# A graph block on one core: keys' and values' products placed between attention's gathers, the next head's maxima spread over a head, rows by DRAM, 16-bit routing

## The chip, the cores and the metric

The kernel runs on one core of one Trainium2 chip. The metric is device time in microseconds (us) of a whole execution. The engines are named as in the profile: PE multiplies matrices (PEld is its weight load), DVE is the vector engine, ACT the scalar engine with the exponential, POOL is GpSimd, SP is the engine that issues most DMAs.

## The reference, cut to what matters

x has 1250 nodes of 768 features, and src, dst hold 41,250 edges. Everything is fp32.

```python
xn = layernorm(x)
# 1. two graph attention layers (4 heads of 192, then 2 of 96), on a second layer norm of xn
h = (x @ W).reshape(n, H, C)
e = leaky_relu(s_src[src] + s_dst[dst], 0.2)      # s_src, s_dst: one number a node and head
ee = exp(e - segment_max(e, dst)[dst])
out = segment_sum(ee / denom[dst] * h[src], dst) + bias
gnn = concatenate([x, out2]) @ Wu + bu
# 2. linear attention, 12 heads of 64, phi = elu + 1
kv, ksum = einsum(phi(k), v), phi(k).sum()
mix = (phi(q) @ kv / (phi(q) @ ksum)) @ Wo + bo
x = x + gnn + mix
# 3. eight experts, two a token, gates not normalised
gate = layernorm(x) @ Wg + bg
scores, idx = top_k(gate, 2)
x = x + sum over the two of score * (gelu(xl @ W1[e] + b1[e]) @ W2[e] + b2[e])
```

## The kernel before, in words

Nodes are cut into ten tiles of 125 (PT, NT). The whole kernel is straight code, traced once; a scheduler orders each engine's instructions by their place in the program and by when it thinks that they are ready. So an instruction can run long before those that are written ahead of it, where its inputs and buffers allow that. The trace shows the order that results.

The stages are these.

1. Edges become a dense matrix of counts AT (source tile by all 1250 targets) and its mask. The normalised nodes, transposed (xnT), are multiplied by weights folded from W1 and W2 (L430), which gives gw, what is gathered, and s1, the two scores of each node and head.
2. Attention, six heads in two layers. `attend` (L495) treats one head. `across` (L497) lays a column of scores over all partitions as a row of 1250: ten PE transposes, up to four in one PSUM bank, three evacuations by ACT. There is one such bank (rb_p, L475). It makes ss_row, the sources' scores less the head's least one. Ten DVE operations (L515) then take, for each target tile, the maximum of ss_row under the mask. From those come two columns, up and dn (L523, L524), and two more rows by `across`. The loop over source tiles st (L528) makes a weight tile w of 125 x 1250: two exponentials on ACT (L533, L534), a maximum and a multiplication by the counts on DVE (L535, L536). w has three buffers, v two. A gather multiplies w on PE: in layer one w is the stationary side, ten blocks times 198 columns (L548); in layer two h2 is (L569). The sums take five PSUM banks in layer one, and after each head DVE adds them, divided by the denominator, into h2 (L555 to L558); after a head of layer two ACT copies them to o2T (L574).
3. Four weight buffers are opened once attention's memory is closed (L581, L584): Wo, Wq, Wu, and a smaller one for the rest of Wu (L591, L593).
4. Keys and values (L598 to L629): for each node tile and half (k) six matmuls for keys, six for values, then three that multiply the two, added to kvacc by DVE. In the trace an fp32 matmul is two instructions, so a half is 12, 12 and 6. Keys pass through elu + 1: add, minimum, an exponential on ACT, maximum and add.
5. kvacc is masked, transposed and multiplied into Wo (L637 to L684).
6. Routing (L768): for each node tile, queries (L751) of the next tile, the output rows po (L781, L792), a layer norm, gates (L810), rank among the eight, and from it counts of earlier nodes per expert (L830, with tri, ones and cum), a place for each of the two choices, and one-hot matrices hot and put (L849, L852), whose product inv (L854) inverts places into node numbers and gates. idx and gs (L859, L861) hold these.
7. Experts (L950): rows of xl_d are gathered from DRAM by idx, transposed, pass two layers, are scaled by gs and added into the output by an indirect DMA.

Of the kernel before, what the change touches and what calls it, by code (L numbers as in the profile page):

```python
# [69 lines left out]
def gps_block(ctx: ExitStack, tc: tile.TileContext, x, src, dst, norm_g, norm_b, W1, a_src1, a_dst1,  # L70
# [60 lines left out]
    xl_d = dram.tile([N + 128, D], F32)  # L131
# [348 lines left out]
    def least(ss, H):  # L480

        mn = small.tile([PT, H], F32, name="mn")
        nc.vector.tensor_reduce(mn, ss.rearrange("p t h -> p h t"), AX.X, ALU.min)
        p = four()
        nc.tensor.transpose(p[:H, 0], mn, ident[:PT, :PT])
        m1 = small.tile([H, 1], F32, name="m1")
        nc.vector.tensor_reduce(m1, p[:H, 0], AX.X, ALU.min)
        p = four()
        nc.tensor.transpose(p[:, 0, :H], m1.to_broadcast([H, PT]), ident[:H, :H])
        lo = small.tile([PT, 2, H], F32, name="lo")  # L490
        nc.vector.tensor_copy(lo[:, 0], p[:, 0, :H])
        nc.vector.tensor_scalar(lo[:, 1], p[:, 0, :H], -1.0, None, op0=ALU.mult)
        return lo

    def attend(ss, sd, lo, wp, rb, gather):  # L495

        def across(cols, name, bufs, bias=0.0):  # L497

            row = rb.tile([PT, N], F32, name=name, bufs=bufs)
            for g0 in range(0, NT, 4):  # L500
                n = min(4, NT - g0)
                p = four()
                for q in range(n):
                    nc.tensor.transpose(p[:, q], cols[:, g0 + q:g0 + q + 1].to_broadcast([PT, PT]),
                                        ident[:PT, :PT])
                nc.scalar.activation(row[:, g0 * PT:(g0 + n) * PT],  # L506
                                     p[:, :n].rearrange("p a b -> p (a b)"), AF.Identity, bias=bias)
            return row


        ss_row = across(ss, "ss_row", 1, lo[:, 1:2])
        top = small.tile([PT, NT], F32, name="top")
        for t in range(NT):
            scr = wp.tile([PT, N], BF16, name="scr", bufs=1)
            nc.vector.tensor_tensor_reduce(scr, ss_row, mask[:, t], 1.0, 0.0, ALU.mult, ALU.max,  # L515
                                           top[:, t:t + 1])

        nc.vector.scalar_tensor_tensor(top, top, lo[:, 0:1], sd, op0=ALU.add, op1=ALU.add)
        nc.vector.scalar_tensor_tensor(top, top, SLOPE, top, op0=ALU.mult, op1=ALU.max)
        up = small.tile([PT, NT], F32, name="up")  # L520
        dn = small.tile([PT, NT], F32, name="dn")
        sl = small.tile([PT, NT], F32, name="sl")
        nc.vector.tensor_sub(up, sd, top)  # L523
        nc.vector.scalar_tensor_tensor(dn, sd, SLOPE, top, op0=ALU.mult, op1=ALU.subtract)  # L524
        nc.vector.tensor_scalar(sl, ss, SLOPE, None, op0=ALU.mult)
        up_row = across(up, "up_row", 1)
        dn_row = across(dn, "dn_row", 1)
        for st in range(NT):  # L528


            w = wp.tile([PT, N], F32, name="w", bufs=3)
            v = wp.tile([PT, N], F32, name="v", bufs=2)
            nc.scalar.activation(w, up_row, AF.Exp, bias=ss[:, st:st + 1])  # L533
            nc.scalar.activation(v, dn_row, AF.Exp, bias=sl[:, st:st + 1])  # L534
            nc.vector.tensor_tensor(w, v, w, op=ALU.max)  # L535
            nc.vector.scalar_tensor_tensor(w, w, 2.0, AT[:, st, :N], op0=ALU.min, op1=ALU.mult)  # L536
            gather(st, w)

    lo1 = least(s1[:, :, :, 0], H1)
    with tc.tile_pool(name="wp", bufs=3) as wp, tc.tile_pool(name="rb", bufs=1) as rb:  # L540
        with tc.tile_pool(name="ag_p1", bufs=1, space=PSUM) as ag_p:
            for hd in range(H1):
                ag = ag_p.tile([PT, NT // 2, 512], F32, name="ag")

                def gather1(st, w):
# [6 lines left out]
                attend(s1[:, :, hd, 0], s1[:, :, hd, 1], lo1[:, :, hd], wp, rb, gather1)  # L552
                v = ag[:, :, :2 * CG].rearrange("p a (b c) -> p a b c", b=2)
                rd = small.tile([PT, NT // 2, 2, 1], F32, name="rd")
                nc.vector.reciprocal(rd, v[:, :, :, C2:C2 + 1])  # L555
                for t in range(NT):
                    nc.vector.scalar_tensor_tensor(h2[:, t], v[:, t // 2, t % 2], rd[:, t // 2, t % 2],
                                                   h2[:, t], op0=ALU.mult, op1=ALU.add)  # L558
# [3 lines left out]
        lo2 = least(h2[:, :, at:at + H2], H2)  # L562
        with tc.tile_pool(name="ag_p2", bufs=1, space=PSUM) as ag_p:
            for hd in range(H2):
                ag = ag_p.tile([C2 + 1, 3, 512], F32, name="ag")

                def gather2(st, w):
                    for i, (a, b) in enumerate(NCH):
                        nc.tensor.matmul(ag[:, i, :b - a], h2[:, st, hd * (C2 + 1):(hd + 1) * (C2 + 1)],  # L569
                                         w[:, a:b], start=st == 0, stop=st == NT - 1)  # L570

                attend(h2[:, :, at + hd], h2[:, :, at + H2 + hd], lo2[:, :, hd], wp, rb, gather2)
                for i, (a, b) in enumerate(NCH):
                    nc.scalar.copy(o2T[:, hd, a:b], ag[:, i, :b - a])  # L574
# [22 lines left out]

    for t in range(NT):  # L598
        ky = kp.tile([PT, D], F32, name="ky", bufs=2)
        va = kp.tile([PT, KC, 129], F32, name="va")  # L600
        nc.gpsimd.memset(va[:, :, 128:], 1.0)
        for k in range(2):
            half = slice(k * 384, (k + 1) * 384)
            for w in (Wk_sb, Wv_sb):
                ps = bank()
                for c in range(KC):
                    nc.tensor.matmul(ps[:PT, :384], xnT[:, c, t * PT:(t + 1) * PT], w[:, c, half],  # L607
                                     start=c == 0, stop=c == KC - 1)
                if w is Wk_sb:
                    ke = kp.tile([PT, 384], F32, name="ke", bufs=1)  # L610
                    nc.vector.tensor_add(ky[:, half], ps[:PT, :384], bk_b[:, half])
                    nc.vector.tensor_scalar(ke, ky[:, half], 0.0, None, op0=ALU.min)
                    nc.scalar.activation(ke, ke, AF.Exp)
                    nc.vector.scalar_tensor_tensor(ky[:, half], ky[:, half], 0.0, ke, op0=ALU.max,
                                                   op1=ALU.add)
                else:
                    nc.scalar.copy(va[:, 3 * k:3 * k + 3, :128],
                                   ps[:PT, :384].rearrange("p (b c) -> p b c", b=3))
            ps = bank()
            for c in range(3):  # L620
                nc.tensor.matmul(ps[:, c * 129:(c + 1) * 129],
                                 ky[:, (3 * k + c) * 128:(3 * k + c + 1) * 128], va[:, 3 * k + c],
                                 start=c == 0, stop=c == 2, skip_group_check=True)
            acc = kvacc[:, 3 * k:3 * k + 3]
            got = ps[:, :387].rearrange("p (b c) -> p b c", b=3)
            if t:
                nc.vector.tensor_add(acc, acc, got)  # L627
            else:
                nc.vector.tensor_copy(acc, got)  # L629
# [56 lines left out]
    zero = fp.tile([128, D], F32)  # L686
    nc.gpsimd.memset(zero, 0.0)
    nc.sync.dma_start(xl_d[N:], zero)
    nc.sync.dma_start(out[N:], zero)
# [4 lines left out]
    gs = fp.tile([128, NV + 1], F32)  # L694
# [4 lines left out]
    with ExitStack() as rs:  # L699
# [7 lines left out]
        def numbers(shape, pattern, base, mult, name):  # L707
            t = rp.tile(shape, F32, name=name)
# [8 lines left out]
        row128 = numbers([PT, 128], [[1, 128]], 0, 0, "row128")  # L717
        steps = numbers([128, NE, NJ - FIX], [[0, NE], [128, NJ - FIX]], 128 * FIX, 0, "steps")
        slot_row = numbers([PT, NV], [[1, NV]], 0, 0, "slot_row")
# [6 lines left out]
        ones = rp.tile([PT, 128], F32)  # L726
        nc.gpsimd.memset(ones, 1.0)
        tri = rp.tile([PT, 128], F32)
# [4 lines left out]
        nc.gpsimd.memset(gs[:, NV:], 0.0)  # L733
# [5 lines left out]
        cum = rp.tile([PT, NT + 1, NE], F32)  # L739
        nc.vector.memset(cum[:, 0], 0.0)  # L740
        inv = g_p.tile([128, 2, NV], F32, name="inv", bufs=1)
# [26 lines left out]
        for t in range(NT):  # L768
# [30 lines left out]
            xl = rl.tile([PT, D], F32, name="xl")  # L799
            normalise(xl, xt)  # L800
            for p, tt in token_rows(t):
                nc.sync.dma_start(xlr[p, tt], xl[p])
# [6 lines left out]
            gate = rl.tile([PT, NE], F32, name="gate")  # L809
            nc.vector.tensor_add(gate, pg[:PT, :NE], bg_b)  # L810

# [11 lines left out]
            sel = rl.tile([PT, NE], F32, name="sel")  # L823
# [10 lines left out]
            two = rl.tile([PT, 2, 2, NE], F32, name="two")  # L834
            for i, a in enumerate((at, gate)):
                nc.vector.tensor_mul(two[:, i], kth, a[:, None, :].to_broadcast([PT, 2, NE]))
            both = rl.tile([PT, 2, 2], F32, name="both")
            nc.vector.tensor_reduce(both, two, AX.X, ALU.add)
            b_i = rl.tile([PT, 2], I32, name="b_i")
            nc.vector.tensor_copy(b_i, both[:, 0])  # L840
# [6 lines left out]
            for k in range(2):  # L847
                hot = rl.tile([PT, 128], F32, name="hot")
                nc.vector.tensor_scalar(hot, row128, s_f[:, 1, k:k + 1], None, op0=ALU.is_equal)  # L849
                put = rl.tile([PT, 2, NV], F32, name="put")  # L850
# [165 lines left out]
```

## Time and profile before

| | |
|---|---|
| Median of 3 runs | 1179.99 us (1179.2 to 1181.08) |
| The profiled execution | 1180.66 us |
| Its span in the trace | 1178.6 us |
| Mean granted clock of PE | 0.971 |
| Busy | PE 91%, PE's loads 61%, DVE 57%, ACT 30%, POOL 6% |

The span is cut as follows by the trace (first starts): edges and features to some 196 us; the first maximum of attention at 220.37; the last gather's end at 593.4; the weights for the output at 612.97; routing to 937; the first gather of tokens at 937.47; experts to the end. The profile gives for each engine what it did and what ended its idle time. A busy PE need not be at its peak, because matmuls overlap: where it is, back-to-back starts tell. A clock below 1.0 means that PE was granted less than full speed.

### The profile page before, as it was taken

The numbers are of one execution on the slowest core, as the hardware profiler recorded it, in microseconds if no ns is written. First come the engines' busy times: TensorE is split into PE (matmuls) and PEld (weight loads), VectorE is DVE, ScalarE is ACT, GpSimd is POOL, SyncE is SP. The second block draws the span as 40 slices with busy tenths as digits, with TensorE's granted clock in tenths as the row PEclk, the third lists the DMA queues.
The fourth block names the chain that finished last, engine by engine and source line by source line (L and its number), as shares of the span: only waits on it lengthen the run. The fifth ranks groups of instructions, "written<-read, shape, count | busy, mean of one in ns | idle before, by whom it ended". The sixth has DMA issues, their size and how long they took to land.

```text
span 1178.6 us, 12106 instructions
## 1 busy us (share of the span) xinstructions
PE 1077.8 (91%) x4583; PEld 723.6 (61%) x4583; DVE 669.1 (57%) x1366; ACT 358.1 (30%) x527; POOL 76.3 (6%) x100
## 2 busy tenths in 40 slices
PE   2599998999999999988989999999999589999993
PEld 2586655578788878544545666666666356666652
DVE  6866666669696966687922555555555422222210
ACT  2131114373737373373712211111111011111111
POOL 1000000000000000000000000000000122322321
PEclk9999998999999999989989999999999789999997
DMA  5014000000000001000083111111123537777533
GB/s 156 27 51 163 16 25 1 1 1 1 1 1 1 1 1 53 1 0 1 1 319 103 40 40 40 40 40 40 39 65 106 191 91 188 200 209 219 121 56 54
DMA packets 33282, 79.62 MB, mean 68 GB/s; under 512 B 5258, under 2 KB 13020, under 8 KB 33208
## 3 DMA queue, kind: packets, MB, share of 16 engines
q1 hardware_dynamic: 27608, 59.02, 15.2%
q0 software_dynamic: 5600, 19.66, 8.4%
q8 instruction: 40, 0.66, 0.2%
q14 instruction: 34, 0.28, 0.1%
HBM read 60.37 MB, written 18.30 MB: 67 GB/s over the span
## 4 chain that ended last, share of the span: by engine, by line
PE 70%; DVE 20%; DMA 5%; issue 2%; ACT 2%; POOL 1%; DVEq 0%; SPq 0%; POOLq 0%; ACTq 0%
PE po L781 13%; PE ph L926 8%; PE py L938 7%; PE mm L430 7%; PE mm L607 7%; PE mm L751 7%; DVE scr L515 6%; DVE w L535 5%; DVE w L536 5%; PE ag L548 3%; PE ag L569 2%; PE u L792 2%; PE px L912 2%; PE mm L405 2%; DMA w<-in_L_gnn_Wu_dram 2%
## 5 line engine op out<-in xcount | busy, mean ns | idle before, releaser
L548 PE MATMUL ag<-kept,w 125*125 125x198 f32 x800 | 137.4, 333 | 5.1 <-DVE w L536 4.9
L548 PEld LDWEIGHTS ag<-kept,w 125*125 125x125 f32 x800 | 133.5, 188 | 9.0 <-DVE w L536 9.0
L926 PE MATMUL ph<-xsT,w 128*128 128x384 f32 (+1 forms) x324 | 100.6, 470 | 1.8 <-DVE xsT L915 1.8
L938 PE MATMUL py<-w,hT 128*128 128x384 f32 x300 | 100.6, 486 | 0.0
L430 PE MATMUL mm<-Wg,xnT 128*125 128x400 f32 x240 | 91.8, 520 | 1.0 <-DVE xnT L321 0.6
L607 PE MATMUL mm<-Wv_sb,xnT 128*125 128x384 f32 x240 | 85.7, 489 | 4.8 <-DVE kvacc L627 4.8
L535 DVE TENSOR_TENSOR w<-v,w 125x1250 f32<-125x1250 f32 x60 | 86.3, 1453 | 6.6 <-ACT w L533 5.9
L515 DVE CUSTOM_DVE_ANT_0 scr<-ss_row,mask 125x1250 bf16<-125x1250 f32 x60 | 87.2, 1453 | 0.5 <-ACT ss_row L506 0.2
L781 PE MATMUL po<-w,xnT 128*125 128x384 f32 x240 | 84.8, 496 | 2.6 <-DMA w<-in_L_gnn_Wu_dram 2.6
L536 DVE SCALAR_TENSOR_TENSOR w<-w,AT 125x1250 f32<-125x1250 f32 x60 | 86.4, 1455 | 0.4
L926 PEld LDWEIGHTS ph<-xsT,w 128*128 128x128 f32 x324 | 59.8, 193 | 41.4 <-DVE xsT L915 2.4
L607 PE MATMUL mm<-Wk_sb,xnT 128*125 128x384 f32 x240 | 84.4, 486 | 0.0
L534 ACT ACTIVATE v<-dn_row,sl 125x1250 f32<-125x1250 f32 x60 | 79.3, 1333 | 16.9 <-DVE w L535 16.4
L751 PE MATMUL mm<-w,xnT 128*125 128x384 f32 x240 | 84.2, 489 | 0.0
L915 DVE COPY xsT<-px 128x384 f32<-128x384 f32 x50 | 25.5, 552 | 99.2 <-PE px L912 77.3
L781 PE MATMUL po<-w,qT 128*125 128x384 f32 x240 | 80.8, 486 | 0.0
L938 PEld LDWEIGHTS py<-w,hT 128*128 128x128 f32 x300 | 55.3, 190 | 33.9
L941 DVE TENSOR_TENSOR ys<-py,wb 128x768 f32<-128x768 f32 x25 | 23.9, 958 | 74.0 <-PE py L938 45.5
L781 PEld LDWEIGHTS po<-w,xnT 128*125 128x125 f32 x240 | 44.2, 190 | 30.1 <-DMA w<-in_L_gnn_Wu_dram 2.8
L781 PEld LDWEIGHTS po<-w,qT 128*125 128x125 f32 x240 | 44.2, 188 | 29.4
L607 PEld LDWEIGHTS mm<-Wv_sb,xnT 128*125 128x125 f32 x240 | 42.4, 187 | 31.1 <-DVE kvacc L627 6.9
L751 PEld LDWEIGHTS mm<-w,xnT 128*125 128x125 f32 x240 | 43.6, 188 | 27.6 <-ACT qT L321 0.2
(274 smaller groups left out, 1415.6 us busy)
## 6 DMA issues: line engine op xcount, KB each, us to landing
w<-in_L_ffn_W_dram SPq DMA_DIRECT2D x18, 1152.0 KB
xt<-in_x_dram SPq DMA_DIRECT2D x20, 336.0 KB
wb<-in_L_ffn_b_dram SPq DMA_DIRECT2D x9, 384.0 KB
out_dram<-xt SPq DMA_DIRECT2D x10, 336.0 KB
xl_d<-xl SPq DMA_DIRECT2D x10, 336.0 KB
W_sb<-in_L_gnn_W_dram SPq DMA_DIRECT2D x1, 2304.0 KB
Wk_sb<-in_L_mix_Wk_dram SPq DMA_DIRECT2D x1, 2304.0 KB
Wv_sb<-in_L_mix_Wv_dram SPq DMA_DIRECT2D x1, 2304.0 KB
```

The source lines that it names most:

```text
L430: nc.tensor.matmul(ps[:PT, :2 * (CG + 2)], xnT[:, c, t * PT:(t + 1) * PT], Wg1[:, c, 2 * k:2 * k + 2].rearrange("p h c -> p (h c)"), start ...
L515: nc.vector.tensor_tensor_reduce(scr, ss_row, mask[:, t], 1.0, 0.0, ALU.mult, ALU.max, top[:, t:t + 1])
L534: nc.scalar.activation(v, dn_row, AF.Exp, bias=sl[:, st:st + 1])
L535: nc.vector.tensor_tensor(w, v, w, op=ALU.max)
L536: nc.vector.scalar_tensor_tensor(w, w, 2.0, AT[:, st, :N], op0=ALU.min, op1=ALU.mult)
L548: nc.tensor.matmul(ag[:, t // 2, o:o + CG], w[:, t * PT:(t + 1) * PT], gw[:, st, hd], start=st == 0 and t % 2 == 0, stop=st == NT - 1, ski ...
L607: nc.tensor.matmul(ps[:PT, :384], xnT[:, c, t * PT:(t + 1) * PT], w[:, c, half], start=c == 0, stop=c == KC - 1)
L751: nc.tensor.matmul(ps[:PT, :384], xnT[:, c, tk], Wq_sb[:, c, half], start=c == 0, stop=c == KC - 1)
L781: nc.tensor.matmul(po[k][:, :384], l, r[:, k * 384:(k + 1) * 384], start=i == 0, stop=i == len(parts) - 1)
L915: nc.vector.tensor_copy(xT[:, 3 * a:3 * a + 3, j * 128:(j + 1) * 128], px[:, a, :384].rearrange("p (b n) -> p b n", b=3))
L926: nc.tensor.matmul(ph[:, :n * 128], w[0][:, o:o + 128], xT[:, c, :n * 128], start=c == 0, stop=c == KC - 1)
L938: nc.tensor.matmul(py[:, k, :384], hT[:, f, j * 128:(j + 1) * 128], w[:, o:o + 384], start=f == 0, stop=f == FC - 1)
```

## The change

- `attend` becomes `layer`, over all heads of a layer. A generator `sides_of(h)` holds a head's maxima, two at a time, then its up and dn columns. The first head's is run through at once; each later head's is stepped once after each source tile of the head ahead of it: two maxima after each of tiles 0 to 4, the columns after tile 5.
- Rows: each layer's scores less the least (over) are transposed once for all heads and written to DRAM (`to_rows`); up and dn of a later head too. Later heads' rows are read back by DMAs that repeat a row over 125 partitions. The first head of each layer still uses `across`. The row buffer holds up and dn together, twice; v has one buffer instead of two.
- Keys and values become a generator of 60 pieces (keys, values, their product, for each half). One piece follows each of layer one's 40 source tiles, and 8 of 10 in each of layer two's heads; the other 4 come after attention. ky is now half a tile, three buffers.
- Routing: row128, slot_row, ones, tri, cum, sel, hot and put are fp16; inv holds node numbers alone. Gates are written beside the rows of xl_d (776 columns instead of 768), and a gather brings them along; a DVE copy takes the expert's column.

```diff
-    xl_d = dram.tile([N + 128, D], F32)
+    row_d = [dram.tile([n * NT, PT], F32, name=f"row{i}") for i, n in enumerate((H1, H2, 2))]
+    xl_d = dram.tile([N + 128, D + NE], F32)
...
+    def to_rows(cols, d):
+        n = cols.shape[1]
+        p = four()
+        nc.tensor.transpose(p[:n, 0], cols, ident[:PT, :PT])
+        r = small.tile([H1 * NT, PT], F32, name="r", bufs=2)
+        nc.scalar.copy(r[:n], p[:n, 0])
+        nc.sync.dma_start(d, r[:n])
...
+    def layer(ss, sd, H, d, wp, rb, head):
+        lo = least(ss, H)
+        over = small.tile([PT, H, NT], F32, name="over", bufs=1)
+        for h in range(H):
+            nc.vector.tensor_scalar(over[:, h], ss[:, :, h], lo[:, h:h + 1], None, op0=ALU.subtract)
+        to_rows(over.rearrange("p h t -> p (h t)"), d)
+
+        def scores(h):
+            ss_row = rb.tile([PT, N], F32, name="ss_row")
+            if h:
+                nc.sync.dma_start(ss_row, row_bcast(d[h * NT:(h + 1) * NT], PT))
+            else:
+                across(over[:, h], ss_row)
+            return ss_row
+
+        def sides_of(h):
+            top = small.tile([PT, NT], F32, name="top")
+            for t in range(NT):
+                scr = wp.tile([PT, N], BF16, name="scr", bufs=1)
+                nc.vector.tensor_tensor_reduce(scr, rows_of[h], mask[:, t], 1.0, 0.0, ALU.mult, ALU.max,
+                                               top[:, t:t + 1])
+                if t % 2:
+                    yield
+            if h + 1 < H:
+                rows_of[h + 1] = scores(h + 1)
...
+            row = rb.tile([PT, 2, N], F32, name="row", bufs=2)
+            if h:
+                to_rows(sides.rearrange("p a t -> p (a t)"), row_d[2])
+                nc.sync.dma_start(row.rearrange("p a n -> p (a n)"), row_bcast(row_d[2], PT))
+            else:
+                for a in range(2):
+                    across(sides[:, a], row[:, a])
+            made[h] = row, sl
+            yield
+
+        made, rows_of = {}, {0: scores(0)}
+        for _ in sides_of(0):
+            pass
+        for h in range(H):
+            row, sl = made[h]
+            ahead = sides_of(h + 1) if h + 1 < H else iter(())
+            gather, finish = head(h)
+            for st in range(NT):
...
+                v = wp.tile([PT, N], F32, name="v", bufs=1)
...
+                gather(st, w)
+                next(ahead, None)
+                if H == H1 or st % 4 != 3:
+                    next(keys, None)
+            finish()
...
+    keys = keys_and_values()
...
+    for _ in keys:
+        pass
...
-        ones = rp.tile([PT, 128], F32)
+        ones = rp.tile([PT, 128], F16)
-        tri = rp.tile([PT, 128], F32)
+        tri = rp.tile([PT, 128], F16)
-        cum = rp.tile([PT, NT + 1, NE], F32)
+        cum = rp.tile([PT, NT + 1, NE], F16)
-        inv = g_p.tile([128, 2, NV], F32, name="inv", bufs=1)
+        inv = g_p.tile([128, NV], F32, name="inv", bufs=1)
...
-            gate = rl.tile([PT, NE], F32, name="gate")
+            gate = xl[:, D:]
             nc.vector.tensor_add(gate, pg[:PT, :NE], bg_b)
+            for p, tt in token_rows(t):
+                nc.sync.dma_start(xlr[p, tt, D:], gate[p])
...
-                hot = rl.tile([PT, 128], F32, name="hot")
+                hot = rl.tile([PT, 128], F16, name="hot")
-                put = rl.tile([PT, 2, NV], F32, name="put")
-                for i, v in enumerate((node1[:, t:t + 1], both[:, 1, k:k + 1])):
-                    nc.vector.tensor_scalar(put[:, i], slot_row, s_f[:, 0, k:k + 1], v,
-                                            op0=ALU.is_equal, op1=ALU.mult)
+                put = rl.tile([PT, NV], F16, name="put")
+                nc.vector.tensor_scalar(put, slot_row, s_f[:, 0, k:k + 1], node1[:, t:t + 1],
+                                        op0=ALU.is_equal, op1=ALU.mult)
...
-        nc.vector.tensor_copy(gs[:, :NV], inv[:, 1])
...
-            xg = sp.tile([128, D], F32, name="xg", bufs=3)
+            xg = sp.tile([128, D + NE], F32, name="xg", bufs=3)
...
+            at = slice(D + e, D + e + 1) if isinstance(e, int) else bass.ds(e + D, 1)
+            nc.vector.tensor_copy(gates[:, j:j + 1], xg[:, at])
```

## The prediction

> **What bounds the kernel now.** I read the page's busy shares, then a table of busy time by stretch, the timeline inside stretches, the chain that ended last, and DMA shares.
>
> The page's first line, then rows of the stretch table (us; busy us and instructions on PE, PE's weight loads, DVE, ACT, POOL; granted clock; DMA share; GB/s):
>
> ```profile
> PE 1077.8 (91%) x4583; PEld 723.6 (61%) x4583; DVE 669.1 (57%) x1366; ACT 358.1 (30%) x527; POOL 76.3 (6%) x100
> ```
> ```profile
> 249.00:291.00 42.00, 40.74 (x229) 37.47 (x228) 41.97 (x43) 23.07 (x22) 0.00 (x0) 1.00 0.00 1
> 291.00:307.00 16.00, 14.00 (x63) 9.14 (x62) 6.51 (x22) 8.30 (x12) 0.11 (x1) 1.00 0.00 1
> 503.00:546.00 43.00, 36.15 (x108) 17.94 (x107) 41.17 (x42) 24.47 (x25) 0.11 (x1) 0.92 0.00 0
> 640.00:920.00 280.00, 279.98 (x1055) 173.42 (x1053) 148.48 (x403) 48.30 (x74) 0.00 (x0) 1.00 0.17 53
> ```
>
> PE looks full everywhere; DVE differs. While a head is gathered (249 to 291) DVE is full: a source tile takes two weight operations and one of the next head's maxima, 4.12 us, against 3.38 us of matmuls. Between heads (291 to 307) DVE idles and PE works on keys and values. A head lasts 58.4 us (first weight operations at 249.29, 307.76, 366.15, 424.55 in the chain). From 640 to 920 PE alone decides.
>
> Why 16 us between heads, in the timeline:
>
> ```profile
> 296.67 0.60 PE L504 MATMUL rb<-ident,up 125*125 125x125 f32 x4
> 297.37 0.59 ACT L506 ACTIVATE up_row<-rb 125x500 f32<-125x500 f32 x1 [0.61 <-PE rb L504]
> 298.40 0.60 PE L504 MATMUL rb<-ident,up 125*125 125x125 f32 x4
> 299.04 0.59 ACT L506 ACTIVATE up_row<-rb 125x500 f32<-125x500 f32 x1 [1.08 <-PE rb L504]
> ```
>
> Transposes and evacuations take turns on one PSUM bank, with products between. The products thus fill gaps already, though written after attention: their line's first matmul starts at 133.1 us. Moving them can't gain their 155 us.
>
> After attention, in the chain, the last gather is followed by weights whose buffers attention's memory held:
>
> ```profile
> 591.29 2.12 PE ag L569 x6
> ...
> 594.49 18.44 DMA w<-in_L_gnn_Wu_dram
> ...
> 621.62 8.05 PE mm L683 x22
> ...
> 630.82 7.29 PE mm L751 x22
> ```
>
> **What the Trainium skill says.** "Perfetto Trace Analysis", Identifying the Most-Contended Engine: matmul busy time doesn't show how near the limit PE is. The trace agrees: L607's mean is 486 ns, yet 12 together take 4.04 us. So I price work by back-to-back rates from the chain: 0.3225 us at 384 columns (16 in 5.16), 0.169 for the first layer's gather (200 in 33.77), 0.35 for the second's (12 in 4.21), 0.108 for a transpose (4 in 0.43).
> "DMA: Bandwidth & Descriptors", Why a DMA increments its semaphore by 16 and not by 1: a transfer uses the largest number of engines up to 16 that divides its outer dimensions, so 5 for 125 partitions. A broadcast of biases to 125 partitions agrees: share 0.33 (5/16 is 0.31), 132 GB/s:
>
> ```profile
> 451.00:452.00 1.00, 1.00 (x8) 1.00 (x7) 0.00 (x0) 1.00 (x1) 0.00 (x0) 1.00 0.33 132
> ```
>
> The same page, Anatomy of one DMA, gives about 2 us of fixed time. No row here isolates it; I use it for rows through DRAM.
> "TensorE: Matmul & The Clock Gate", Weight-path perf modes: weights other than fp32 load faster at 128 columns. The trace points that way at 125: L465's bf16 loads, 9 in 0.60 us, against 0.19 each in fp32.
>
> **The change, part by part.** All sums are against the profiled execution: 1180.66 us, of which 1178.6 is span and 2.06 lies around it. It is 0.67 above the median 1179.99.
>
> 1. **Three later heads of layer one.** Maxima go two per source tile into tiles 0 to 4; rows come by DMA, so the 16 us ping-pong goes. What is late next is DVE: ten tiles of 4.12 is 41.2, the head's sums 3.6, the small sides 1.2. Products: a "piece" is a third of a half tile: (24 x 0.3225 + 0.75)/3 = 2.83 us of PE, 0.67 us of DVE. With 6 pieces DVE needs 41.2 + 3.6 + 1.2 + 4 = 50.0, PE 33.8 + 1 + 17 = 51.8. I take 53, with 1.2 for hand-over; ends are 50 and 58.4 (nothing won). 3 x (58.4 - 53) = **-16.2**.
> 2. **Rows through DRAM.** Sides for two rows: 125 x 10,000 B = 1.25 MB at 132 GB/s is 9.5 us, the score row half of that, 4.7, ahead of it on the same engines. With two fixed 2 us, small operations, a transpose and a copy (2.5), that is 21 us at worst, about 17 where the score row overlaps the write. It starts after tile 4; five tiles remain, 5 x 3.4 = 17 where PE sets the pace, 14 where DVE does, then 4 of sums. So it just fits; I charge 3 us once, in layer two, where no product is left to cover it. Ends 0 and 7 a head (four heads). Issues are six small writes and eight reads on SP, whose queue held only four bias loads here. The one shared v buffer makes ACT's second exponential wait for DVE's maximum; an exponential is 1.33 and the next DVE operation 1.45, so 0 to 0.2 a tile, behind PE.
> 3. **Last head of layer one, start of layer two.** Before: 424.55 to 503.02, 78.5. Layer one's 40 tiles carry a piece each, so 40 pieces must be done by its end. Some 15 are done by 249 (6 before 220, 9 after) and 18 in three heads; 7 remain, 20 us: 33.8 + 20 = 54. Then layer two's opening (sums, least, score row, ten maxima, sides) stays 40 and takes 12 pieces. 94: **+15.5**. But 52 of 60 pieces are then done, where 44.7 were: paid back below.
> 4. **Layer two.** Before 503.02 to 593.4, 90.4. After: first head on DVE 47 (41.2 + 1.2 + 8 pieces, 5), copies 3, last head 20 x 1.37 and its waits 30, rows 3 from point 2: 83. **-7.4**. PE has 42 + 23 in it, below DVE. All products may then be done.
> 5. **Weights' wait.** Wo, Wq, Wu land at 18.4 after issue whatever PE does. Before, PE filled that with products, then ran L675, L683 and the first queries: 593.4 to 638.1, 44.7. After, the products are gone, and L683 (7.7) may start when the first third of the weights is there, 7 us on; queries (7.7), L675 (2.6), six po (1.9) follow: 27, plus 5.5 for a clock lowered by the idle start (0.5 from 612 to 618 now). 32.5: **-12.2**. Ends: -16, and 0 if the order doesn't bring L683 forward.
> 6. **Routing.** In a steady round:
>
> ```profile
> 732.36 1.45 PE L781 MATMUL po<-w,xnT 128*125 128x384 f32 x4
> 733.65 0.29 PE L830 MATMUL g<-sel,tri 125*128 125x8 f32 x2
> 733.79 0.37 PE L830 MATMUL g<-cum,ones 125*128 125x8 f32 x2
> 734.01 2.83 PE L781 MATMUL po<-w,xnT 128*125 128x384 f32 x8
> 736.68 0.84 PE L854 MATMUL inv<-put,hot 125*128 125x160 f32 x4
> 737.35 4.04 PE L781 MATMUL po<-w,xnT 128*125 128x384 f32 x12
> ```
>
> Counts occupy 734.01 - 733.65 = 0.36, inverse 737.35 - 736.68 = 0.67. Half as many instructions remain, on 80 columns, loads perhaps half: I take 0.3 for both, between 0.1 and 0.6. 9 x 0.73 = **-6.5**. The last tile is a bare chain: two put operations (0.46) and some 1.1 of matmuls at a clock of 0.5: **-1.6**. The dropped gate product and copy hide beside PE: 0. Gates as 32-byte writes, twenty on SP: ready at 928.8, landing about 933 behind weights that end near 931.5, first gather at 937.5: 0, up to +4 if late. Gate copies after gathers, 0.15 us on a DVE idle there; rows of 3,104 bytes for 3,072: 0.
>
> Sum: -16.2 + 15.5 - 7.4 - 12.2 - 6.5 - 1.6 = -28.4; 1180.66 - 28.4 = 1152.3, and against the median **1152**. Cross-check from PE: 120 transposes less (-13), six more (+0.7), routing -8, make -20; the other 8 is idle filled, of about 45 between 220 and 638 (417 us, 372 of work at back-to-back rates).
>
> **Rivals.** *PE was full already*: the products filled gaps before, so moving them is no change, and only removed PE work counts: 1180 - 20 = **1160**. For it: L607 between heads; against it: DVE's 10 idle us a head. *Nearly no idle left*: heads at 50 (-9 more) and the weights' wait at -16 (-4), rows in time (-3): **1136**. For it: both engines have room between heads; against it: DVE full at 503 to 546. *Rows late, slower*: two weight steps (5.5) and queued exponentials (4) ahead of the sides make 21 into 30, 11 beyond the latest cover. Four heads lose 44: 1152 + 44 = **1196**. It decides from 7 us a head (4 x 7 = 28). Against it: remaining products cover PE.
>
> **Numbers.** Forecast 0.50 (1143 to 1159), PE full 0.22, nearly no idle 0.17, rows partly late and within 0.2% of no change 0.04, slower 0.07. About 0.2% is what a measurement here can tell. Range 1135 to 1168: it leaves out the late-row cases and the far edge of the good one. Faster 0.89, same 0.04, slower 0.07.
>
> **What would show it.** Heads 53 apart; 60 row transposes instead of 180; DVE without its gap between heads; L683 inside the weights' wait; routing rounds of 28.8 instead of 29.5; the first token gather some 7 us after the last gates (8.85 now). Wrong if heads stay near 58, if first exponentials wait on rows by DMA, if products are left over after attention, or if token gathers wait for gates.

## The result, and the profile after

The changed kernel takes **1188.63 us** (median of 6 runs, 1186.33 to 1189.58), the kernel before 1180.09 beside it (1176.61 to 1182.83): ratio **1.0075, 95% interval 1.006 to 1.009**. It is slower; the forecast was 1152. The profiled execution took 1189.58 us, its span 1187.8; its mean clock is 0.949, where 0.971 was granted before. In the code after the change the row write is L502, `across` L510 and L512, the score row's read L525, a maximum L537, the double row's read L555, the two exponentials L574 and L575, DVE's weight steps L576 and L577, products L595 and L611, gathers L631 and L656, the sums after a head L638 and L640, the fold of Wo (before: L683) L743, queries L810, output rows L840, counts L891, the inverse L913. Below, a score row is ss_row; a double row is `row`, which holds a head's up and dn; products are those of keys and values; a hole is a stretch in which an engine stands idle.

The page's first line:

```profile
PE 1059.5 (89%) x4428; PEld 706.3 (59%) x4428; DVE 668.0 (56%) x1363; ACT 343.6 (29%) x497; POOL 76.4 (6%) x99
```

PE does 18 us less than before (1077.8), about the 20 of the cross-check, in a span that is 9 us longer. So time is lost in holes, not in work. The table cuts both traces, and those of two experiments told below, at the same events: first starts, and the end of a layer's last gather. The first row is nearly the same work in all four, and two traces of the same code differ there by 3.1 us (217.1 with rows on PE, 220.2 with the fold first as well), so the other rows are the ones to compare.

| us | before | after | rows over 128 partitions | rows on PE |
|---|---|---|---|---|
| to the first maximum | 220.4 | 221.9 | 221.7 | 217.1 |
| first head, to its sums' reciprocal | 69.3 | 82.4 | 73.0 | 74.7 |
| three later heads, to the last reciprocal | 172.8 | 183.7 | 179.0 | 178.4 |
| opening of layer two, to its first gather | 44.8 | 51.8 | 48.9 | 47.1 |
| gathers of layer two | 86.1 | 71.2 | 64.8 | 63.8 |
| weights' wait, fold, first queries | 44.7 | 46.7 | 45.2 | 45.5 |
| output rows, routing, experts | 540.5 | 530.2 | 528.9 | 528.6 |

From before to after, layer one and layer two's opening lose 31 us, the gathers of layer two win 15, the weights' wait loses 2, and the last row, with routing in it, wins 10.

The chain of waits (start, us, what) shows the first cause, which the kernel before did not have:

```profile
283.37 1.25 DMA row<-r
284.63 12.88 DMA row<-row
...
403.67 13.02 DMA row<-row
```

A double row takes 12 to 13 us from issue to use, four times. The timeline shows what that does at the first change of head (a bracket is the engine's idle time before, and who ended it):

```profile
297.60 1.34 ACT L574 ACTIVATE w<-row,s 125x1250 f32<-125x1250 f32 x1 [8.68 <-DMA row<-row]
...
300.20 1.46 DVE L576 TENSOR_TENSOR w<-v,w 125x1250 f32<-125x1250 f32 x1 [5.78 <-ACT v L575]
...
305.77 3.40 DVE L640 SCALAR_TENSOR_TENSOR h<-ag,rd,h 125x198 f32<-125x198 f32 x10
...
309.22 3.00 PE L631 MATMUL ag<-kept,w 125*125 125x198 f32 x8 [11.13 <-DVE h L640]
```

ACT waits 8.68 us for the row. DVE's next instruction is the new head's weight step, which waits for ACT; the old head's sums (L640) stand behind it on DVE's queue, though the last gather that they read ended at 298.1. The new head's gathers need the sums done, because one PSUM tile serves both heads, so PE stands for 11.13. No product fills that hole. The program steps one after each source tile, but the scheduler's order puts them ahead of that head's gathers and none beside them. The keys' and values' instructions (L595) alone, from the first maximum to 370 (stretch, us, PE busy and instructions, loads, clock, DMA share, GB/s):

```profile
221.90:258.40 36.50, 25.23 (x75) 13.15 (x73) 0.95 0.05 18
258.40:309.20 50.80, 0.00 (x0) 0.00 (x0) 0.90 0.10 38
309.20:370.20 61.00, 18.21 (x54) 9.83 (x54) 0.94 0.09 31
```

The stretch table, in the columns that the prediction used, answers to the rows of before for 249 to 307:

```profile
258.40:300.00 41.60, 36.72 (x201) 34.72 (x201) 36.02 (x38) 22.29 (x18) 0.00 (x0) 0.96 0.12 46
300.00:309.20 9.20, 0.00 (x0) 0.00 (x0) 9.00 (x17) 5.30 (x5) 0.00 (x0) 0.63 0.00 0
```

Before, DVE idled between heads and PE worked on products. Now, from 300 to 309, DVE works alone, PE does nothing, and its clock falls to 0.63.

ACT's later stalls for double rows are 6.18, 7.21 and 6.34. Twice DVE waits for a score row as well, 5.35 and 5.15 us, because the next head's maxima stand ahead of this head's weight steps on its queue; the first of them:

```profile
246.02 1.46 DVE L537 CUSTOM_DVE_ANT_0 scr<-ss_row,mask 125x1250 bf16<-125x1250 f32 x1 [5.35 <-DMA ss_row<-row]
```

The weights' wait, in the chain:

```profile
623.70 10.21 DMA Wg_sb<-in_L_ffn_Wg_dram
633.91 2.88 PE po L840 x4
636.80 2.72 PE mm L735 x8
...
641.15 8.05 PE mm L743 x22
```

L743, the fold of Wo, runs after the weights have landed, behind two groups that need the last of them. PE stands for 10.69 us ahead of the first of the two, where it stood 2.57 before. Routing, in a steady round:

```profile
780.24 0.17 PE L891 MATMUL g<-sel,tri 125*128 125x8 f16 x1
780.27 0.17 PE L891 MATMUL g<-cum,ones 125*128 125x8 f16 x1
780.29 2.18 PE L840 MATMUL po<-w,xnT 128*125 128x384 f32 x6
782.31 0.20 PE L913 MATMUL inv<-put,hot 125*128 125x80 f16 x1
782.35 0.88 PE L840 MATMUL po<-w,xnT 128*125 128x384 f32 x2
```

Counts now occupy 780.29 - 780.24 = 0.05 us, where it was 0.36, and each of two inverse products 0.04, where the four took 0.67. Rounds last 28.77 instead of 29.54.

### The profile page after: what moved, and what is told of

The parts are those of the page before. It is cut to its first block, busy times and chain, and to the rows that moved or that the text cites. A ratio compares the mean times of both kernels' runs of the same rounds, so it can differ in the third digit from the quotient of the medians.

```text
span 1187.8 us, 11866 instructions
## 1 busy us (share of the span) xinstructions
PE 1059.5 (89%) x4428; PEld 706.3 (59%) x4428; DVE 668.0 (56%) x1363; ACT 343.6 (29%) x497; POOL 76.4 (6%) x99
## 4 chain that ended last, share of the span: by engine, by line
PE 72%; DVE 12%; DMA 8%; issue 3%; ACT 2%; POOL 0%; DVEq 0%; SPq 0%; POOLq 0%; ACTq 0%
PE po L840 13%; PE ph L985 8%; PE mm L595 8%; PE mm L431 7%; PE py L997 7%; PE mm L810 7%; PE ag L631 6%; DMA row<-row 4%; DVE scr L537 4%; DVE w L576 2%; DVE w L577 2%; PE u L851 2%; PE ag L656 2%; PE mm L406 2%; PE px L969 2%
## 5 line engine op out<-in xcount | busy, mean ns | idle before, releaser
L631 PE MATMUL ag<-kept,w 125*125 125x198 f32 x800 | 144.8, 339 | 20.2 <-DVE h L640 11.1
L631 PEld LDWEIGHTS ag<-kept,w 125*125 125x125 f32 x800 | 138.9, 193 | 27.6 <-DVE w L577 11.6
L576 DVE TENSOR_TENSOR w<-v,w 125x1250 f32<-125x1250 f32 x60 | 87.3, 1455 | 35.6 <-ACT w L574 22.0
L575 ACT ACTIVATE v<-row,sl 125x1250 f32<-125x1250 f32 x60 | 80.2, 1337 | 81.0 <-DVE w L576 67.4
L537 DVE CUSTOM_DVE_ANT_0 scr<-ss_row,mask 125x1250 bf16<-125x1250 f32 x60 | 87.3, 1455 | 13.5 <-DMA ss_row<-row 10.5
L840 PE MATMUL po<-w,xnT 128*125 128x384 f32 x240 | 84.4, 501 | 10.7 <-DMA Wg_sb<-in_L_ffn_Wg_dram 10.7
L577 DVE SCALAR_TENSOR_TENSOR w<-w,AT 125x1250 f32<-125x1250 f32 x60 | 87.3, 1456 | 0.7
L595 PE MATMUL mm<-Wk_sb,xnT 128*125 128x384 f32 x240 | 86.0, 497 | 0.0
L810 PE MATMUL mm<-w,xnT 128*125 128x384 f32 x240 | 84.2, 489 | 0.0
L595 PE MATMUL mm<-Wv_sb,xnT 128*125 128x384 f32 x240 | 84.0, 487 | 0.0
L840 PE MATMUL po<-w,qT 128*125 128x384 f32 x240 | 80.8, 487 | 0.0
L840 PEld LDWEIGHTS po<-w,xnT 128*125 128x125 f32 x240 | 43.3, 190 | 38.9 <-DMA Wg_sb<-in_L_ffn_Wg_dram 10.8
L574 ACT ACTIVATE w<-row,s 125x1250 f32<-125x1250 f32 x40 | 53.4, 1334 | 40.9 <-PE ag L631 32.2
L840 PEld LDWEIGHTS po<-w,qT 128*125 128x125 f32 x240 | 44.1, 188 | 29.5 <-issue 0.2
L595 PEld LDWEIGHTS mm<-Wv_sb,xnT 128*125 128x125 f32 x240 | 43.6, 187 | 27.9 <-issue 3.2
```

Source lines behind the costliest of these rows:

```text
L537: nc.vector.tensor_tensor_reduce(scr, rows_of[h], mask[:, t], 1.0, 0.0, ALU.mult, ALU.max, top[:, t:t + 1])
L574: nc.scalar.activation(w, row[:, 0], AF.Exp, bias=ss[:, st, h:h + 1])
L575: nc.scalar.activation(v, row[:, 1], AF.Exp, bias=sl[:, st:st + 1])
L631: nc.tensor.matmul(ag[:, t // 2, o:o + CG], w[:, t * PT:(t + 1) * PT], gw[:, st, hd], start=st == 0 and t % 2 == 0, stop=st == NT - 1, ski ...
L810: nc.tensor.matmul(ps[:PT, :384], xnT[:, c, tk], Wq_sb[:, c, half], start=c == 0, stop=c == KC - 1)
L840: nc.tensor.matmul(po[k][:, :384], l, r[:, k * 384:(k + 1) * 384], start=i == 0, stop=i == len(parts) - 1)
```

## The experiments

Theory L: rows come late, for an instruction order that is fixed as if they came early. Rival P: the products and the spread maxima stand in the wrong places, whatever the rows do. Rival C: the lower clock is a cause of its own. The kernel before, run beside each of them, took 1177.7 to 1180.1; ratios are against it, with 95% intervals.

| kernel | us | ratio |
|---|---|---|
| changed kernel | 1188.63 | 1.0075 (1.006 to 1.009) |
| rows over 128 partitions | 1161.85 | 0.985 (0.983 to 0.987) |
| double rows alone over 128 | 1169.35 | 0.992 (0.990 to 0.995) |
| no products stepped, rows late | 1206.55 | 1.022 (1.020 to 1.024) |
| routing part alone on before | 1166.48 | 0.989 (0.987 to 0.991) |
| rows on PE | 1159.53 | 0.983 (0.981 to 0.985) |
| rows on PE, no products stepped | 1168.06 | 0.991 (0.989 to 0.993) |
| rows on PE, maxima even over the head | 1168.10 | 0.990 (0.988 to 0.992) |
| rows on PE, fold first | 1151.82 | 0.976 (0.973 to 0.978) |
| rows over 128, fold first | 1155.15 | 0.980 (0.977 to 0.983) |
| before with routing, fold first | 1164.11 | 0.986 (0.984 to 0.988) |

**Rows over 128 partitions.** The changed kernel with

```diff
-            ss_row = rb.tile([PT, N], F32, name="ss_row")
+            ss_row = rb.tile([128, N], F32, name="ss_row")
...
-                nc.sync.dma_start(row.rearrange("p a n -> p (a n)"), row_bcast(row_d[2], PT))
+                nc.sync.dma_start(row.rearrange("p a n -> p (a n)"), row_bcast(row_d[2], 128))
```

and the same for the other read and buffer; users take the first 125 partitions.

> The changed kernel with its row buffers and broadcast reads over 128 partitions instead of 125, so that a read can use 16 DMA engines instead of 5; every engine's instructions stay in the same order. Theory L (rows come late for an order that is fixed for early rows): the double-row reads fall from 12 to 13 us to 4 to 6, the score-row reads from 6 to 7 to 3 to 4; the four stalls of the exponentials (8.7, 6.2, 7.2, 6.3) and the two of the maxima (7.3, 6.2) mostly go, and the kernel is at 1160 to 1168. Rival P (the products are in the wrong places, or the later maxima run ahead of the first weights, rows or not): the stalls go but DVE's and PE's order gives most of it back, 1178 to 1188. Rival C (the lower granted clock is a cause and not an effect): the clock stays near 0.95 and the time stays above 1183.

It took 1161.85, **26.8 us** below the changed kernel; by the traces every engine's instructions stand in the same order. The stretch table while the first double row travels, the changed kernel first (stretch, us, PE, loads, DVE, ACT, POOL, clock, DMA share, GB/s):

```profile
286.00:297.00 11.00, 9.75 (x55) 9.14 (x56) 8.42 (x9) 2.00 (x2) 0.00 (x0) 1.00 0.29 111
```
```profile
281.50:286.00 4.50, 3.55 (x21) 3.31 (x20) 4.50 (x5) 2.68 (x2) 0.00 (x0) 1.00 0.83 280
```

A share of 0.29 for 125 partitions and 0.83 for 128, edges of the transfer included, fits the rule of the Trainium skill, "DMA: Bandwidth & Descriptors", Why a DMA increments its semaphore by 16 and not by 1: the engine count has to divide the partitions, so 5 of 16 (0.31) against all 16. The read takes 6.0 us instead of 12.9, and ACT waits little:

```profile
286.95 1.34 ACT L574 ACTIVATE w<-row,s 125x1250 f32<-125x1250 f32 x1 [1.74 <-DMA row<-row]
```

That is L. P had 1178 to 1188, C above 1183. The mean clocks of the five runs are 0.956 to 0.971, those of the changed kernel's six 0.949 to 0.965: a run of the changed kernel at 0.965 took 1186.33, one with wider reads at 0.956 took 1163.44. So the clock doesn't make the difference; C falls.

PE's hole at the first change of head is 5.26 us now instead of 11.13. DVE starts the old head's sums as soon as the last gather ends, but PE still has nothing to do beside them:

```profile
299.65 0.69 PE L631 MATMUL ag<-kept,w 125*125 125x198 f32 x1 [5.26 <-DVE h L640]
```

**Double rows alone over 128.** The edit above without the score row's half.

> The changed kernel with only the four double-row reads over 128 partitions; the four score-row reads stay on 125. It splits the 26.8 us that both together gave. Theory L says a head pays for a row in proportion to how far its read overruns the tiles left: the double rows stalled the exponentials by 28.4 in sum, the score rows stalled the maxima by 13.5, in the trace of the changed kernel. If both kinds count by their stalls, this one gets 28.4 of 41.9, two thirds: 1168 to 1174. If only the double rows count (the score-row stall hides beside TensorE's products), 1161 to 1164. If the score rows are what pushes everything back, above 1178.

1169.35, inside L's range: 19.3 of the 26.8 us belong to the double rows, 7.5 to the score rows, good to some 3 us, for the six runs spread from 1165.19 to 1172.38. The expectation put the score rows' stalls at 13.5, which is how long their reads took in the chain (7.34 and 6.20); DVE itself stood idle for 5.35 + 5.15 = 10.5. Stalls of 28.4 and 10.5 share the 26.8 as 19.6 and 7.2.

A microsecond of stall in the changed kernel thus cost 0.69 us (26.8 of 38.9) on average, but not evenly. By the stage table the first head, with stalls of 8.68 and 5.35 and no product in it, gets back 9.4 us with wider reads, and layer two's gathers, with 6.34, get back 6.4. The three later heads, with 6.18 and 7.21 and products in all of them, get back only 4.7.

**No products stepped.** The changed kernel, rows late, without the step in the loop over source tiles:

```diff
-                if H == H1 or st % 4 != 3:
-                    next(keys, None)
```

> The changed kernel with no product stepped into a head; all are written after attention, as in the kernel before, and fill gaps where the engine order finds them. Rows through DRAM and spread maxima stay. Theory L: the rows are as late as in the changed kernel, so the heads still stall and the time stays at 1180 to 1195. Rival P: 1165 to 1175, since the products now cover the holes.

1206.55, **17.9 slower** than the changed kernel and above both ranges. Products in the scheduler's own places don't cover the holes: of the 480 instructions of keys and values, 13 lie between the sums of layer one's first head and those of its last, where the changed kernel has 193, and 199 come after the last gather, where it has 17. Stepping them was no fault; P falls.

**Routing alone.** The kernel before with the routing lines of the diff and nothing else.

> The kernel before with only the routing part of the change: 16-bit one-hots and counts, gates kept in the token rows. All theories: routing saves what the stage showed, 9 to 10 us from the first steady round to the first token gather, less about 1 at the start: 1170 to 1173. If it gives 1178 or more, the routing part is not what made that stage shorter. The prediction's terms for it were 6.5 and 1.6.

1166.48, 12.9 below before, more than expected. By the two traces 9.8 lie between the first long run of output rows (638.11 before) and the first gather of tokens, 1.6 after it, 1.3 ahead; that much is there at the first maximum already, in work that the edit doesn't touch. So the rest of the change costs 1188.63 - 1166.48 = **22.2 us**.

**Rows on PE.** The changed kernel with no row through DRAM:

```diff
-            if h:
-                nc.sync.dma_start(ss_row, row_bcast(d[h * NT:(h + 1) * NT], PT))
-            else:
-                across(over[:, h], ss_row)
+            across(over[:, h], ss_row)
```

and so for the double rows.

> The changed kernel with every row made on TensorE by transposes, as before the change, and none sent through DRAM; products stay stepped into the heads, maxima stay spread, routing stays 16-bit. The instruction order is made anew. Theory L: a row costs about 13 us of transposes and copies in turn, but maxima are spread, so it overlaps tiles: 1168 to 1182, below the changed kernel by 7 to 20. Rival P: above 1183, as slow as the changed kernel or slower, since 120 transposes (13 us) come back.

1159.53: below my range, and 2.3 us below the rows over 128 partitions that ran beside it, with all five runs (1157.21 to 1160.19) below all of theirs (1161.19 to 1163.44). So taking 120 transposes off PE by way of DRAM has won nothing, and here cost some 2 us. It is not the rows alone that differ, for the instruction order is made anew: it places products beside DVE's sums at the first change of head, and PE stands for 0.53 us there instead of 5.26:

```profile
291.05 0.83 PE L603 MATMUL mm<-va,ky 125*128 125x129 f32 x6
291.71 0.60 PE L510 MATMUL rb<-ident,over 125*125 125x125 f32 x4
292.15 4.04 PE L587 MATMUL mm<-Wk_sb,xnT 128*125 128x384 f32 x12
296.71 3.62 PE L623 MATMUL ag<-kept,w 125*125 125x198 f32 x20 [0.53 <-DVE h L632]
```

**Rows on PE, no products stepped,** and **rows on PE, maxima even.** The first leaves the step of the keys out. The second takes the spread back:

```diff
-                if t % 2:
-                    yield
+                yield
...
+            for _ in ahead:
+                pass
             finish()
```

> The kernel with rows made on TensorE, and no product stepped into a head (all written after attention, as in the kernel before). What is left of the change is the spread maxima and the routing. Against the routing alone (1166.5) it measures the spread; against rows on TensorE with stepped products (1159.5) it measures the stepping. If stepping is worth what it was with late rows (18 us), 1175 to 1180; if the products filled the gaps by themselves, as the prediction's first rival has it, 1158 to 1163. I expect 1165 to 1172.

> The kernel with rows made on TensorE and products stepped into the heads, but the next head's maxima again one per source tile over all ten tiles (as in the kernel before), its sides and rows after the last tile. It takes the spread alone back from the kernel of 1159.5. If early maxima matter only because they let a row be made inside a head, the 16 us of transposes and copies in turn stand between the heads again, filled only by what products find there: 1164 to 1172. If stepping alone carries the gain, as the pair without stepping suggests (1168.1 with early maxima, 1166.5 without), 1157 to 1162.

With the routing kernel they make a square: neither 1166.5, spread alone 1168.1, stepping alone 1168.1, both 1159.5. Neither alone can be told from no gain; **only both together win 7**. The square is not quite clean: the corner with neither also keeps the buffers of before, two of v and one set of rows, which no run takes apart. Why spread alone wins nothing, its stretch after attention shows:

```profile
535.50:640.00 104.50, 99.78 (x343) 56.57 (x341) 27.49 (x59) 18.65 (x47) 3.20 (x18) 1.00 0.36 119
```

With the maxima spread and no products between, later heads last 44.6, 46.0 and 38.8 us, and the last gather ends at 535.5, 58 us earlier than before. Then PE is busy for 99.78 of 104.5 us: 185 of the 480 instructions of keys and values are still to do, where routing alone leaves 29.

Stepping alone does the opposite: one of the 480 is left after the last gather. Attention takes no less time for it (372.6 us from the first maximum to the last gather, 373.0 with routing alone), and PE then stands until the last large weight lands:

```profile
611.84 2.92 PE L833 MATMUL po<-w,xnT 128*125 128x384 f32 x4 [14.87 <-DMA w<-in_L_gnn_Wu_dram]
```

The 28 instructions that moved, some 9 us by the price of 0.3225, came out of a wait that lasts as long without them: 20.8 us from the last gather to the first output rows, 20.1 with routing alone.

**Fold first.** On rows on PE, on rows over 128, and on before with routing, the loop of L743 is written ahead of the bias product that needs the last weight:

```diff
+    for c in range(KC):
+        for k in range(2):
+            half = slice(k * 384, (k + 1) * 384)
+            ps = bank()
+            nc.tensor.matmul(ps[:, :384], kvT[:, c], Wo_sb[:, c, half], start=True, stop=True)
+            nc.scalar.copy(Wo_sb[:, c, half], ps[:, :384])
     nc.gpsimd.tensor_add(bu_b, bu_b, bo_b)
     for k in range(2):
```

and taken out behind it.

> The kernel with rows made on TensorE, and the fold of Wo (the 24 instructions of 384 columns that the prediction's step 5 wanted inside the weights' wait) written ahead of the bias product that needs the last of the four weights. On TensorE's queue it then stands ahead of the first product of the last large weight. If step 5 failed because of the order alone, the fold (7.7 us) moves into the 19 us wait and the time falls from 1159.5 to 1151 to 1154. If Wo comes no earlier than the others (all four weights share the engines), the fold waits with them: 1158 to 1160.

> The changed kernel, rows through DRAM over 128 partitions, and the fold of Wo ahead of the bias product. Rows in time (1161.9) less the fold (7.7): 1152 to 1156. That would be the prediction's sum with its two failed steps mended, row reads and place of the fold. If the two interact (the weights' DMAs behind row DMAs on SP's queue), 1157 to 1162.

> The kernel before with the routing part, and the fold of Wo written ahead of the bias product; attention as before the change. In that kernel products of keys and values are left over for the weights' wait, so there are two readings. If the wait is not filled by them anyway (they end long before the last weight lands), the fold gains what it gained with rows on TensorE, 7.7: 1157 to 1161. If the leftover products fill it, as the prediction said of the kernel before, the fold gains less than 3: 1163 to 1167.

1151.82 (7.7 won), 1155.15 (6.7 won), 1164.11 (2.4, intervals overlap). The chain with rows on PE, whose last gather ends at 584.27:

```profile
587.96 6.01 PE mm L587 x18
...
598.48 8.87 PE mm L726 x24
607.35 1.29 PE po L831 x4
```

The fold (L726 there) now stands inside the wait: PE goes from it to the first output rows at 607.35 without a stop, where with rows on PE it stood 6.24 us for the last large weight. In the kernel before with routing, whose last gather ends at 591.83, leftover products come first:

```profile
596.58 7.76 PE mm L607 x24
...
608.84 8.87 PE mm L674 x24
617.71 2.58 PE po L779 x8
```

so much of the wait was already filled, as the prediction had said of before. The first of the three is the fastest kernel of all these.

## Why the prediction was wrong

**The step that failed is point 2, "so it just fits".** Taken apart at the first change of head: columns ready at 279.30, row in use at 297.60, 18.3, within my 17 to 21. But the prediction started that at the last maximum, and the small operations stood between weight steps on DVE: from the last maximum's end (273.43) to the columns are 5.9 more, 24.2 in all. The read alone was 12.9, not 9.5 + 2: it moved 111 GB/s in the stretch shown (122 from 286 to 296), where I took 132 from a bias load. Against it stood what was left of the exponentials, 15.5 us to their end at 288.92, not 17 + 4: sums give ACT no cover, as they run on DVE behind the new head's step. The row overran its cover by 8.7. The charge of 3 us once should have been about the 26.8 that the wider reads gave back. The prediction had the five engines of a 125-partition read in its price and never asked what 128 partitions would cost.

**The rival with 0.07 was the case.** "Rows late, slower" had 1196 and a deciding point of 7 us a head. ACT's stalls were 6.2 to 8.7 a head and the time 1188.6. Its mechanism held and its price was high: it had 30 from the last maximum to the row where 24.2 were measured, and a stall cost 0.69 of itself. What I set against it, "remaining products cover PE", was half true: it held in the later heads, which have products and lost 4.7 for 13.4 of stall, and failed in the first, which has none and lost 9.4 for 14.0. A product covers a hole only where the fixed order places it.

**Points 1, 3 and 4** summed to -8.1 from the first maximum to the last gather. With rows in time they measured 365.7 - 373.0 = -7.3 (128 partitions) and 364.0 - 373.0 = -9.0 (PE). The sum was right, but by luck, for the split was not. By the prediction's own marks, the first weight step of each head, rows over 128 give -24.3 for point 1 (heads 40.2, 50.4 and 60.3 apart, where it had 53), +36.7 for point 3 and -19.5 for point 4, where it had -16.2, +15.5 and -7.4. The heads' first weight steps run ahead of their gathers: from sums to sums the later heads lasted 57.1, 62.5 and 59.4, with up to 78 instructions of L595 in one, where the six pieces are 48. In the changed kernel the sum was +16.0.

**Point 5** promised -12.2, and 0 "if the order doesn't bring L683 forward". It didn't: 46.7 after, 45.2 and 45.5 with rows in time. Written first, the fold brought 6.7 and 7.7; it began 14.2 us after the last gather rather than 7, behind 24 product instructions and the masks and transposes of kvacc. The 24 are of the four pieces that the change leaves for after attention; the prediction had counted the products as gone. So some 7 of the 12.2 were a matter of order, and the rest was promised too much.

**Point 6** had the mechanism right and its size low: -6.5 became 9 x 0.77 = -6.9, the last tile's -1.6 became -2.6 (gates' start to first gather 11.5 before, 9.0 with routing alone), and what follows won 1.6 more. The 0.3 us left for counts and inverse is 0.05 + 2 x 0.04 = 0.13, with loads of 0.098 us for 0.189 each, the half that was taken as perhaps. A round should then have shrunk by 0.90; the difference seems to stand in the output rows behind them, six in 2.04 us and two in 0.72, where 0.3225 each gives 1.94 and 0.65. Gates were not late: the first gather comes 6.4 us after them.

**The sum, mended.** Reads over 128 partitions and the fold in its place: 1155.15, beside the forecast of 1152 and inside the stated 1135 to 1168. Of the "PE full already" rival the square shows half: heads that are some 13 us shorter win nothing while the products stay outside them. Two things stay open. Stepping alone empties the weights' wait, but whether the fold written first would turn that into time was not tried. And of the hole of 11.13 us the late row made some 5.9, by the 5.26 left with rows over 128; whether the sums placed ahead of the new head's weight step would do the same with late rows was not tried either.

## What to carry to other kernels

A row, or any transfer, that is to be hidden needs its whole path timed against its cover: from the last instruction that feeds it, with what is queued between, to its use, and at the rate that its partition count gives. Where an order is fixed, cover counts only if the covering instructions are placed in the hole, and what stands behind the waiting instruction on its queue waits too. Freeing an engine brought time here only where other work that still had to be done was moved into what was freed.

## What was not expected of the hardware

- The same row over 128 partitions instead of 125: 280 GB/s against 111, 6.0 us against 12.9, 2.5 times the rate for 16 engines against 5 (3.2 times as many).
- A write of 20 rows of 125 numbers to DRAM took 1.25 us until the read behind it was issued, below the 2 us of fixed time that I had taken from the Trainium skill, "DMA: Bandwidth & Descriptors", Anatomy of one DMA, whose section is on DMAs that GpSimd issues, while SP issues these. The read behind it took 12.9, of which 1.25 MB at 122 GB/s is 10.2 by estimate.
- A 16-bit product is one instruction where fp32 is two, and on 8 columns the two counts occupied 0.05 us where the four fp32 instructions took 0.36.
- The changed kernel's PE, with its hole of 11.13 us from 298 to 309, was granted 0.62 of full speed from 300 to 310 and 0.87 from 310 to 320. With rows over 128, whose hole of 5.26 us ends at 299.65, it was 0.71 and then 1.00; with rows on PE, whose hole there is 0.53, it was 1.00 in both.
